# A relational graph layer on one core: message tiles that SyncE fetched row by row are gathered by GpSimd again

## The chip, the cores and the metric

The kernel runs on one core of a Trainium2 chip. The metric is the time of one execution on the device in microseconds (us). Five engines take part, each with its own queue of instructions: PE (TensorE, matrix products; PEld is its loading of weights), DVE (VectorE), ACT (ScalarE), POOL (GpSimd) and SP (SyncE, which here only issues transfers). Transfers (DMA) run beside them on 16 DMA engines and are issued from SP's queue and from POOL's.

## The reference

12,500 nodes with 256 features each; 212,500 edges, sorted by the node they lead to (`dst`), of which the last one of each node is its loop to itself; each edge has one of 8 types. Layer norm and relu, then one weight matrix per type, then a sum over the edges into each node, and a residual:

```python
def _L0_gnn_ref(edge_index, x, edge_type, weight, h_bias, loop_weight):
    src, dst = (edge_index[0], edge_index[1])
    hx = jnp.einsum('ni,rio->rno', x, weight)
    msg = hx[edge_type, src]
    agg = jax.ops.segment_sum(msg, dst, num_segments=num_nodes)
    node_repr = agg * jnp.asarray(ALPHA, x.dtype) ** 0.5
    node_repr = node_repr + h_bias
    loop_message = x @ loop_weight
    node_repr = node_repr + loop_message * jnp.asarray(1.0 - ALPHA, x.dtype) ** 0.5
    return node_repr

h = jnp.maximum(_layernorm(x, axis=-1), 0.0)
x = x + _L0_gnn_ref(edge_index, h, edge_type_8, L0_gnn_weight, L0_gnn_h_bias, L0_gnn_loop_weight)
```

## The kernel before

The kernel sums first and multiplies later: for every node and every type it adds up the normalized rows `h` of the sources, and only these sums meet the weights.

**Tiles.** An edge tile is 128 edges, one per partition. Two tiles make a unit (`PAIR = 2`), 128 units make a block of indices. There are 1603 tiles, 802 units and 7 blocks. From the second block on a unit covers 267 consecutive edges: the loop edges at the ends of nodes are taken out and come in by another way (`begin`, L799), and the others are moved together into the unit's 256 places. `prepare(b)` (L624) does this for one block on DVE, a few instructions per tile, starting 184 tiles ahead of the block's first tile; it leaves, among others, `gidx[b]`, the source rows of the block's tiles, one column of 128 row numbers per tile.

**Gather.** `gather(t)` (L687) brings the 128 source rows of tile t, 1 KB each, into a message buffer: one indirect transfer issued by POOL (L703), with a column of `gidx` as row numbers. The first 96 tiles read raw `x` rows and normalize them on the spot, since the table `h32` in DRAM isn't complete yet; all others read `h32`. The buffers are pairs of tiles, `MSGS // PAIR` = 30 of them. The main loop calls `gather(t + AHEAD)` at tile t with `AHEAD = 58`, so a gather takes the buffer of the pair 30 pairs earlier, and POOL waits there until PE has read it.

**The single rows.** For one tile in 64 (t % 64 = 63, from the second block on, except the last 58 tiles: tiles 319, 383, ..., 1535, 20 in all) `gather` issues nothing on POOL. It puts eight jobs into the list `fetches`, one for each 16 rows. `load_sources` (L707) loads 16 row numbers from `single[b]`, a copy of the second halves of the units' sources, into registers of SP (L710), and puts 16 transfers of one row each into the list, each addressed by a register (L714). `fetch(3)` (L717, called at L1068) does three entries of the list at each tile.

**Sums.** `onehots(t)` (L721) makes the 0/1 matrices of four tiles on DVE by comparing the edges' places with a row of numbers. `edge_sums(t)` (L747) multiplies the message rows with them on PE into `ps` (L757; four matmul records per tile), and `add_sums(u)` (L765) adds a unit's `ps` to a ring of sums in SBUF, `acc`, on DVE (L769).

**Products.** When the last unit of a group of 128 nodes is in, `group_work(g)` (L904) puts 18 products (L917, 36 records) with the weights into a queue. The main loop spreads them over the following tiles; `finish` (L925) adds the rows of `x` and stores the result from SP's queue (L931, L934).

**Order.** Everything is issued in program order by the loop `for t in range(NT)` from L1064, and each engine works its queue in that order. SP's queue holds the index loads, the row loads of `x` and `h` for groups of nodes (L873), the stores of results and the single rows.

Of the kernel before, what the change touches and what calls it, by code (L numbers as in the profile page):

```python
# [11 lines left out]
I32 = mybir.dt.int32  # L12
# [6 lines left out]
DVE = mybir.EngineType.DVE  # L19

P = 128
SP = mybir.EngineType.SP
EPS = 1e-5
ALPHA = 0.5

# [14 lines left out]
CLEARED = 3  # L40
RING = GROUP * SLOTS

MSGS = 60
AHEAD = 58


# [10 lines left out]

ROWS = 6
FIRST = 4


SINGLE = 64
FETCH = 3
SOURCES = 16

LATE = 8

# [148 lines left out]
def kernel(  # L216
# [11 lines left out]
    nc = tc.nc  # L228
    N, D = x.shape
# [7 lines left out]
    NT = plan.NT  # L237
    U = PAIR * P
# [11 lines left out]
    h32 = dram.tile([N, D], F32, name="h32")  # L250
# [20 lines left out]
    def place_of(t):  # L271
        u, i = divmod(t, PAIR)
        return u // P, i, u % P


    with ExitStack() as main:
# [6 lines left out]
        idx = main.enter_context(tc.tile_pool(name="idx", bufs=2))  # L283
        cols = main.enter_context(tc.tile_pool(name="cols", bufs=3))
        small = main.enter_context(tc.tile_pool(name="small", bufs=4))
        msgs = main.enter_context(tc.tile_pool(name="msgs", bufs=MSGS // PAIR))
        ohs = main.enter_context(tc.tile_pool(name="ohs", bufs=2 + LEAD // QUAD))
# [14 lines left out]

        outs = [ps_o.tile([P, 2, D], F32, name=f"po{i}") for i in range(2)]
        msg, oh, offsets, kind = {}, {}, {}, {}
        single, fetches = {}, []
        firsts, stops, loops, marked, typed, gidx, col = {}, {}, {}, {}, {}, {}, {}
        added, zeroed = {}, {}
        state = {"h32": None}
# [28 lines left out]
        def turned(got, cols, to):  # L337

            def turn():
                pt = ps_d.tile([P, 512], F32, tag="pt", name="ptr")  # L340
                for i in range(PAIR):
                    half = slice(i * P, (i + 1) * P)
                    nc.tensor.transpose(pt[:, half], got[cols][:, half], ident)  # L343
                nc.vector.tensor_copy(to(), pt[:, :U])  # L344

            return [turn]

        def work_tile(got, name, tag, dtype=F32, n=EDGES):
            got[name] = ep.tile([P, n], dtype, tag=f"work{tag}", name=name)
            return got[name]  # L350

        def compacted(got, bit, bits):

            def step(k):
                m = work_tile(got, "moves", 5, I32)
                nc.vector.tensor_single_scalar(m, packed, 1 << (bit + k), op=ALU.bitwise_and)  # L356
                nc.vector.copy_predicated(  # L357
                    packed[:, : EDGES - (1 << k)], m[:, 1 << k :], packed[:, 1 << k :])

            return [lambda k=k: step(k) for k in range(bits)]  # L360

        def kept_sources(b, got):

            def keep():
                single[b] = idx.tile([P, P], I32, name="single")
                nc.vector.tensor_copy(single[b], got["sf"][:, P:U])

            return [] if b == 0 else [keep]

        def sources(b, got):  # L370


            if b == 0:
                def copy():
                    nc.vector.tensor_copy(work_tile(got, "sf", 2)[:, :U], got["s"][:, :U])

                return [copy, *turned(
                    got, "sf", lambda: gidx.setdefault(b, idx.tile([P, U], I32, name="gidx")))]

            def rises():  # L380
                nc.vector.tensor_tensor(
                    work_tile(got, "rise", 0), got["d"][:, 1:], got["d"][:, :EDGES], op=ALU.subtract)

            def stays():
                nc.vector.tensor_scalar(
                    work_tile(got, "stay", 1), got["rise"], 0.0, None, op0=ALU.is_equal)
                firsts[b] = small.tile([P, 1], F32, name="firsts")
                nc.vector.tensor_copy(firsts[b], got["d"][:, 0:1])

            def shifts():  # L390
                nc.vector.scalar_tensor_tensor(
                    work_tile(got, "code", 2), got["d"][:, :EDGES], firsts[b], got["stay"],
                    op0=ALU.subtract, op1=ALU.mult)

            def codes():
                nc.vector.scalar_tensor_tensor(
                    got["code"], got["code"], float(R), got["t"][:, :EDGES], op0=ALU.mult, op1=ALU.add)

            def packs():
                nc.vector.scalar_tensor_tensor(  # L400
                    packed, got["s"][:, :EDGES], float(1 << (TB + SB)), got["code"],
                    op0=ALU.mult, op1=ALU.add)

            def unpacks():
                nc.vector.tensor_single_scalar(
                    work_tile(got, "from", 5, I32)[:, :U], packed[:, :U], TB + SB,
                    op=ALU.logical_shift_right)
                nc.vector.tensor_scalar(  # L408
                    work_tile(got, "sf", 2)[:, :U], got["from"][:, :U], 0.0, float(N - 1),
                    op0=ALU.max, op1=ALU.min)  # L410
                nc.vector.tensor_single_scalar(
                    work_tile(got, "rest", 3, I32)[:, :U], packed[:, :U], (1 << (TB + SB)) - 1,
                    op=ALU.bitwise_and)

            return [rises, stays, shifts, codes, packs, *compacted(got, TB, SB), unpacks,
                    *turned(got, "sf", lambda: gidx.setdefault(b, idx.tile([P, U], I32, name="gidx"))),
                    *kept_sources(b, got)]

        def last_edges(b, got):

# [203 lines left out]
        def prepare(b):  # L624

            got = {}
            return [
                lambda: got.update(load_indices(b)), *sources(b, got), *last_edges(b, got),
                *columns(b, got), *places(b, got), *(verdict(got) if b == NB - 1 else [])]
# [57 lines left out]
        def gather(t):  # L687
            if t % PAIR == 0:
                both = msgs.tile([P, PAIR, D], F32, name="msg")
                for i in range(PAIR):  # L690
                    msg[t + i] = both[:, i, :]
            if t % QUAD:
                kind[t] = kind[t - 1]
            else:
                kind[t] = "h" if state["h32"] is not None and t >= state["h32"] + LATE else "x"
            table = {"h": h32, "x": x}[kind[t]]
            b, i, u = place_of(t)
            if b and i and kind[t] == "h" and t % SINGLE == SINGLE - 1 and t + AHEAD < NT:
                for r in range(0, P, SOURCES):
                    fetches.append(lambda r=r: load_sources(t, r))  # L700
                return
            at = i * P + u
            nc.gpsimd.indirect_dma_start(  # L703
                out=msg[t], out_offset=None, in_=table[:, :],
                in_offset=bass.IndirectOffsetOnAxis(ap=gidx[b][:, at : at + 1], axis=0))

        def load_sources(t, r0):  # L707

            b, _, u = place_of(t)
            _, vals = nc.values_load_multi_w_load_instructions(  # L710
                single[b][u : u + 1, r0 : r0 + SOURCES], engines=[SP], min_val=0, max_val=N - 1,
                skip_runtime_bounds_check_because="clamped to the table where they are computed")
            for i, v in reversed(list(enumerate(vals))):
                fetches.insert(0, lambda i=i, v=v: nc.sync.dma_start(  # L714
                    msg[t][r0 + i : r0 + i + 1, :], h32[bass.ds(v, 1), :]))

        def fetch(n):  # L717
            for _ in range(min(n, len(fetches))):
                fetches.pop(0)()

        def onehots(t):  # L721

# [140 lines left out]
        got = {}  # L863
# [98 lines left out]
        with tc.manual_schedule():  # L962
# [16 lines left out]
            nc.vector.memset(ones_b, 1.0)  # L979
            nc.vector.memset(zero, 0.0)  # L980
            head = len(sources(0, {}))
            for f in load[1 : 1 + head]:
                f()
            for t in range(min(AHEAD, NT)):
                gather(t)
# [49 lines left out]
            def blocks_ahead(t):  # L1035
                for b in range(1, NB):
                    if t == max(0, U * b - PREP):
                        for k, f in enumerate(prepare(b)):
                            background.append((t + STEP * (k // OPS), f))
                        background.sort(key=lambda a: a[0])  # L1040
# [23 lines left out]
            for t in range(NT):  # L1064
                done["tile"] = t
                if t + AHEAD < NT:
                    gather(t + AHEAD)
                fetch(FETCH)  # L1068
                blocks_ahead(t)
                for f in after:  # L1070
                    f()
# [30 lines left out]
                while queue and (budget > 0 and t >= queue[0][0] or t >= queue[0][1]):  # L1102
                    _, _, c, f = queue.pop(0)
# [4 lines left out]
                while waiting and (len(waiting) > LAG or t == NT - 1):  # L1108
                    u, ps = waiting.pop(0)
# [54 lines left out]
```

## Time and profile before

| | |
|---|---|
| time, median of 3 runs | 2032.05 us (2030.82 to 3686.84) |
| time of the profiled execution | 2030.82 us |
| its span, first to last instruction | 2029.1 us |
| granted TensorE clock, mean over the span | 0.945 |
| gathers by POOL (L703) | 96 of `x` and 1487 of `h32` |
| single rows by SP (L714) | 2560 transfers of 1.0 KB, 160 register loads (L710) |
| DMA queues, share of 16 engines' span | 35.0% POOL's, 11.1% SP's |

The profile is one execution, recorded by the hardware profiler. A busy time is the time in which an engine executes an instruction; what its sequencer does for itself (waiting, branching, handing a transfer over) isn't counted as busy. "idle before, releaser" is the time in which the engine stood before an instruction, and what ended it; "issue" there means that the profile shows nothing that it waited for. A row of a timeline gives the start, the duration, the instruction, and the idle time ahead of it in brackets.

### The profile page before, as it was taken

How to read it: one execution, taken by the hardware profiler on the slowest of the kernel's cores; microseconds unless marked ns; L12 is line 12 of the kernel's file. 1: busy time of each engine (PE TensorE's matmuls, PEld its weight loads, DVE VectorE, ACT ScalarE, POOL GpSimd, SP SyncE). 2: the span in 40 equal slices, each digit the busy share in tenths (PEclk: the TensorE clock that was granted, in tenths of full speed). 3: DMA queues.
4: the chain of work that ended last, by engine and by line, in shares of the span. 5: the costliest groups of instructions: out<-in, count | busy, mean ns of one | idle time of the engine just before them, and what ended most of it. 6: DMA issues, size and time to landing. Idle time of an engine off the chain costs nothing.

```text
span 2029.1 us, 37425 instructions
## 1 busy us (share of the span) xinstructions
PE 1784.7 (88%) x10411; PEld 1627.0 (80%) x10411; DVE 1324.2 (65%) x3281; ACT 218.4 (11%) x470; POOL 1504.2 (74%) x1609
## 2 busy tenths in 40 slices
PE   2458999997999997999997989897998898899998
PEld 2357899987989886989886989776898787788886
DVE  7859666658666659656568666557665567765642
ACT  7855110000000000000000000000000000000000
POOL 7757777777777777777777777777777777777773
PEclk8569999998999998999998999999999999999999
DMA  8973443444444444444444444434344444444442
GB/s 293 374 224 105 140 125 117 139 128 125 129 138 120 138 134 121 127 140 118 129 138 127 128 118 138 129 117 146 112 133 129 118 139 130 118 138 123 119 119 72
DMA packets 151127, 281.70 MB, mean 139 GB/s; under 512 B 30365, under 2 KB 100260, under 8 KB 150916
## 3 DMA queue, kind: packets, MB, share of 16 engines
q0 software_dynamic: 75984, 207.59, 35.0%
q1 hardware_dynamic: 74932, 71.68, 11.1%
q8 instruction: 85, 1.39, 0.3%
q14 instruction: 126, 1.03, 0.2%
HBM read 253.55 MB, written 25.60 MB: 138 GB/s over the span
## 4 chain that ended last, share of the span: by engine, by line
PE 33%; SPq 24%; issue 14%; DMA 11%; DVE 11%; POOL 4%; ACT 2%; DVEq 0%; ACTq 0%; POOLq 0%
SPq L714 19%; PE ps L757 17%; PE po L917 15%; DMA msg<-h,gidx 5%; SPq L710 5%; POOL msg L703 4%; DVE acc L769 2%; DMA xr<-in_x_dram 1%; DVE moves L356 1%; DVE fixed L357 1%; DMA h<-xt 1%; DVE oh L730 1%; DMA hr<-h 1%; DVE acc L807 1%; DMA msg<-h 1%
## 5 line engine op out<-in xcount | busy, mean ns | idle before, releaser
L703 POOL DMA_INDIRECT msg<-h,gidx x1487 | 1411.4, 949 | 467.8 <-issue 387.2
L757 PE MATMUL ps<-oh,msg 128*128 128x176 f32 (+1 forms) x6412 | 1151.5, 310 | 168.9 <-ACT msg L661 62.8
L757 PEld LDWEIGHTS ps<-oh,msg 128*128 128x128 f32 x6412 | 1047.5, 197 | 287.8 <-issue 84.2
L917 PE MATMUL po<-w,acc 128*128 128x256 f32 x3136 | 890.6, 386 | 0.0
L730 DVE TENSOR_TENSOR oh<-fixed,cols 128x704 f32<-128x704 f32 x402 | 355.8, 886 | 337.7 <-PE ps L757 328.3
L917 PEld LDWEIGHTS po<-w,acc 128*128 128x128 f32 x3136 | 543.3, 194 | 28.6 <-issue 5.2
L769 DVE TENSOR_TENSOR acc<-acc,ps 128x352 f32 x802 | 412.9, 515 | 158.6 <-PE ps L757 147.7
L807 DVE SCALAR_TENSOR_TENSOR acc<-types,pst 128x256 f32<-128x256 bf16 (+1 forms) x688 | 234.9, 414 | 95.5 <-ACT self_t L796 94.4
L796 ACT ACTIVATE self_t<-pst 128x256 f32<-128x256 f32 x98 | 37.4, 382 | 1470.5 <-PE pst L793 1470.5
L703 POOL DMA_INDIRECT msg<-in_x_dram,gidx x96 | 90.9, 947 | 31.1 <-issue 25.6
L917 PE MATMUL po<-wl,self_t 128*128 128x256 f32 x392 | 106.6, 396 | 3.9 <-ACT self_t L796 2.4
L917 PEld LDWEIGHTS po<-wl,self_t 128*128 128x128 f32 x392 | 70.0, 199 | 10.3 <-ACT self_t L796 2.8
L661 ACT ACTIVATE xt<-xt,n_shift,n_rstd 128x256 f32<-128x256 f32 x98 | 50.9, 588 | 11.0 <-DVE n_shift L658 11.0
L661 ACT ACTIVATE msg<-msg,e_shift,e_rstd 128x256 f32<-128x256 f32 x96 | 49.6, 588 | 8.6 <-DVE e_shift L658 8.6
L928 DVE TENSOR_TENSOR xr<-xr,po 128x256 f32<-128x256 f32 x98 | 40.4, 412 | 7.8 <-PE po L917 7.8
L852 ACT ACTIVATE diagonal<-ident,kinds 128x128 bf16<-128x128 f32 x88 | 28.1, 390 | 149.7 <-DVE kinds L849 149.7
L929 DVE TENSOR_TENSOR xr<-xr,po 128x256 f32<-128x256 f32 x98 | 41.2, 421 | 3.4
L793 PE MATMUL pst<-ident,hr 128*128 128x128 f32 x196 | 38.8, 281 | 1.7 <-DVE cols L344 1.7
L356 DVE TENSOR_SCALAR moves<-fixed 128x267 int32<-128x267 int32 x84 | 36.3, 432 | 1.6
L357 DVE COPY_PREDICATED fixed<-moves,fixed 128x266 int32<-128x266 int32 (+6 forms) x84 | 33.7, 401 | 2.9
L649 DVE BATCH_NORM_STATS2 n_stats<-xt 128x6 f32<-128x256 f32 x98 | 34.4, 411 | 0.9 <-issue 0.7
L343 PE MATMUL ptr<-ident,sf 128*128 128x128 f32 x14 | 4.5, 421 | 33.5 <-DVE sf L408 30.2
(201 smaller groups left out, 351.6 us busy)
## 6 DMA issues: line engine op xcount, KB each, us to landing
msg<-h SPq DMA_DIRECT2D x2560, 1.0 KB
msg<-h,gidx POOLq DMA_INDIRECT x1487
xt<-in_x_dram SPq DMA_DIRECT2D x24, 512.0 KB
h<-xt SPq DMA_DIRECT2D x24, 512.0 KB
xr<-in_x_dram SPq DMA_DIRECT2D x24, 512.0 KB
hr<-h SPq DMA_DIRECT2D x24, 512.0 KB
out_dram<-xr SPq DMA_DIRECT2D x24, 512.0 KB
w<-in_L_gnn_weight_dram SPq DMA_DIRECT2D x2, 1024.0 KB
```

The lines of the kernel that those rows point to most:

```text
L356: nc.vector.tensor_single_scalar(m, packed, 1 << (bit + k), op=ALU.bitwise_and)
L357: nc.vector.copy_predicated(packed[:, : EDGES - (1 << k)], m[:, 1 << k :], packed[:, 1 << k :])
L661: nc.scalar.activation(rows_[j], rows_[j], AF.Relu, bias=shift[:n, j : j + 1], scale=rstd[:n, j : j + 1])
L703: nc.gpsimd.indirect_dma_start(out=msg[t], out_offset=None, in_=table[:, :], in_offset=bass.IndirectOffsetOnAxis(ap=gidx[b][:, at : at + 1 ...
L710: _, vals = nc.values_load_multi_w_load_instructions(single[b][u : u + 1, r0 : r0 + SOURCES], engines=[SP], min_val=0, max_val=N - 1, skip ...
L714: fetches.insert(0, lambda i=i, v=v: nc.sync.dma_start(msg[t][r0 + i : r0 + i + 1, :], h32[bass.ds(v, 1), :]))
L730: nc.vector.tensor_tensor(o[:, k : k + v, :i, :], iota_f.unsqueeze(1).unsqueeze(1).to_broadcast([P, v, i, C]), of.unsqueeze(3).to_broadcas ...
L757: nc.tensor.matmul(ps[:, c, from_ : from_ + width], m[:, c * P : (c + 1) * P], o[:, :width], start=(i == 0 and c == 0), stop=(end and c == ...
L769: i = nc.vector.tensor_tensor(a, a, ps, op=ALU.add)
L807: i = nc.vector.scalar_tensor_tensor(acc[:, :, r, s0 : s0 + n], of, float(r + 1), pst[:, :, :n], op0=ALU.is_equal, op1=ALU.mult)
L917: i = nc.tensor.matmul(got["out", g][:n], lhs, rhs, start=(r == R and c == 0), stop=(r == R - 1 and c == KC - 1))
L929: nc.vector.tensor_add(rows_[:n, k, :], rows_[:n, k, :], got["out", g][:n])
```

## The change

Three things. The tiles with t % 64 = 63 are no longer an exception: `gather` issues an indirect transfer on POOL for each of the 1603 tiles. With the single rows go `load_sources`, `fetch`, the list, and the six copies `single`. And `MSGS` is 62 in place of 60, which makes 31 message buffers of two tiles; `AHEAD` stays 58.

```diff
-MSGS = 60
+MSGS = 62
 AHEAD = 58
...
-SINGLE = 64
-FETCH = 3
-SOURCES = 16
...
-        def kept_sources(b, got):
-
-            def keep():
-                single[b] = idx.tile([P, P], I32, name="single")
-                nc.vector.tensor_copy(single[b], got["sf"][:, P:U])
-
-            return [] if b == 0 else [keep]
...
-                    *turned(got, "sf", lambda: gidx.setdefault(b, idx.tile([P, U], I32, name="gidx"))),
-                    *kept_sources(b, got)]
+                    *turned(got, "sf", lambda: gidx.setdefault(b, idx.tile([P, U], I32, name="gidx")))]
...
-            if b and i and kind[t] == "h" and t % SINGLE == SINGLE - 1 and t + AHEAD < NT:
-                for r in range(0, P, SOURCES):
-                    fetches.append(lambda r=r: load_sources(t, r))
-                return
...
-        def load_sources(t, r0):
-
-            b, _, u = place_of(t)
-            _, vals = nc.values_load_multi_w_load_instructions(
-                single[b][u : u + 1, r0 : r0 + SOURCES], engines=[SP], min_val=0, max_val=N - 1,
-                skip_runtime_bounds_check_because="clamped to the table where they are computed")
-            for i, v in reversed(list(enumerate(vals))):
-                fetches.insert(0, lambda i=i, v=v: nc.sync.dma_start(
-                    msg[t][r0 + i : r0 + i + 1, :], h32[bass.ds(v, 1), :]))
-
-        def fetch(n):
-            for _ in range(min(n, len(fetches))):
-                fetches.pop(0)()
...
-                fetch(FETCH)
```

In the built program PE and ACT execute the same numbers of instructions, DVE six fewer, POOL 20 gathers more (1507 of `h32`), and SP 198 rows of instructions where it had 5478.

More of the change, by code (lines that the diff above doesn't have):

```diff
@@ L21 @@
 P = 128
-SP = mybir.EngineType.SP
 EPS = 1e-5
@@ L304 @@
         msg, oh, offsets, kind = {}, {}, {}, {}
-        single, fetches = {}, []
         firsts, stops, loops, marked, typed, gidx, col = {}, {}, {}, {}, {}, {}, {}
```

## The prediction

> **What bounds the kernel now.** The page comes first: which engine is busiest, and what chain of work ended last.
>
> ```profile
> PE 1784.7 (88%) x10411; PEld 1627.0 (80%) x10411; DVE 1324.2 (65%) x3281; ACT 218.4 (11%) x470; POOL 1504.2 (74%) x1609
> ...
> PE 33%; SPq 24%; issue 14%; DMA 11%; DVE 11%; POOL 4%; ACT 2%; DVEq 0%; ACTq 0%; POOLq 0%
> ```
>
> Read by these lines, PE is the bound, SP's queue (the single rows) carries a quarter of the chain, and POOL hardly matters. Both are to be doubted. Busy is not the same as occupied: handing over a transfer isn't counted. And the chain follows one releaser at each step, so a tile that came from SP leads it into SP's queue for as long as SP was issuing. The test is whether an engine ever waits for another. So the second view is POOL's timeline, in the middle of the run, where nothing is special:
>
> ```profile
> 601.99 0.95 POOL L703 DMA_INDIRECT msg<-h,gidx  x1 [0.30 <-issue]
> 603.24 0.95 POOL L703 DMA_INDIRECT msg<-h,gidx  x1 [0.30 <-issue]
> 604.49 0.94 POOL L703 DMA_INDIRECT msg<-h,gidx  x1 [0.30 <-issue]
> 605.74 0.95 POOL L703 DMA_INDIRECT msg<-h,gidx  x1 [0.30 <-issue]
> ```
>
> A gather starts every 1.25 us: 0.95 busy, 0.30 of handing over. The third view, POOL's waits from 250 us to 2003 us (total, times, longest), says whether it is ever more than that:
>
> ```profile
> POOL msg L703 <- issue: 360.5, 1183, 0.3
> POOL msg L703 <- PE ps L757: 39.9, 131, 0.3
> POOL msg L703 <- DMA msg<-h,gidx: 13.1, 43, 0.3
> ```
>
> No wait is longer than 0.3 us, so the engines named there hold nothing up: from 250 us on POOL gathers without a pause. Whether PE depends on it shows in the records made up to a time; the first four rows are POOL's gathers, the others PE's tile matmuls at L757, four per tile:
>
> ```profile
> 0.00:250.00 250.00, 174.57 (x185) 0.76 0.71 229
> 0.00:800.00 800.00, 591.11 (x623) 0.90 0.53 160
> 0.00:1700.00 1700.00, 1272.22 (x1341) 0.94 0.48 143
> 0.00:2000.00 2000.00, 1499.40 (x1580) 0.94 0.47 140
> ```
> ```profile
> 0.00:250.00 250.00, 113.63 (x528) 104.21 (x528) 0.76 0.71 229
> 0.00:800.00 800.00, 444.47 (x2436) 412.92 (x2437) 0.90 0.53 160
> 0.00:1700.00 1700.00, 974.10 (x5421) 892.28 (x5422) 0.94 0.48 143
> 0.00:2000.00 2000.00, 1147.20 (x6388) 1043.65 (x6388) 0.94 0.47 140
> ```
>
> At 250 us 185 tiles are gathered and 528/4 = 132 are multiplied: 53 in stock. At 800 us it is 623 and the 5 tiles from SP so far, less 609: 19. At 1700 us 1341 + 17 - 1355 = 3, at 2000 us 1580 + 20 - 1597 = 3. Between 250 and 800 us PE takes 1908/4 = 477 tiles, one per 1.15 us, while POOL makes one per 1.25. PE eats the stock up and then goes at POOL's pace. **POOL's issue of gathers is the bound of the whole run**; PE's 88% is what its work looks like when it is fed just in time.
>
> After the last gather comes a tail:
>
> ```profile
> 2002.87 0.95 POOL L703 DMA_INDIRECT msg<-h,gidx  x1 [0.30 <-issue]
> ...
> 2004.20 0.83 PE L757 MATMUL ps<-oh,msg 128*128 128x176 f32 x4 [0.43 <-DMA msg<-h,gidx]
> ...
> 2016.71 7.07 PE L917 MATMUL po<-w,acc 128*84 128x256 f32 x32
> ```
>
> From 2004.20 on PE has the products of the last groups before it; they, an addition and a store end at 2029.1. So the run is: first gather at 4.76, 1582 intervals between gathers, and 2029.1 - 2002.87 = 26.2 us of tail; the execution's own time is 1.7 us more than its span (2030.8).
>
> **Part by part.** *20 more gathers on POOL.* From the gather at 251.12 us to the one at 367.36, before SP issues its first single row, 93 intervals take 1.250 us each; from 1917.84 to 2002.87, after the last one, 68 take 1.250. The 20 additional ones each lie on the path, since nothing else is late on it: 20 x 1.250 = **+25.0 us**. They pull 2.6 MB over from SP's queue to POOL's; the 16 engines are about 45% busy in this stretch, so the bytes are costed at nothing.
>
> *The single rows off SP's queue.* 2560 transfers, each with two register instructions ahead (0.22 + 0.04 + 0.03 us), and 160 loads of 1.28 us: 0.74 + 0.20 ms of SP's time. SP waits for nobody on the path; behind its rows stood only the index loads, the group rows and the stores. The index loads matter to POOL through `gidx`, but the closest case has it written at 187.8 us for a gather at 339.9. PE waited 30.4 us in 8 places for single rows (longest 6.1); that goes, but PE is faster than POOL by 0.1 us per tile and has made the wait good within some 60 tiles; the last such tile, 1535, lies 67 ahead of the end. So this is worth nothing in itself. What may be worth something is the disturbance of POOL: between 369.86 and 1915.33 us its 1232 intervals average 1.2544, and its few long ones (a gather of 1.48 us instead of 0.95 at 475.13) lie in this stretch alone. 1232 x 0.0044 = 5.4 us. That the rows cause it isn't shown, only the coincidence in time; the bounds are 0 and -5.4. I take **-4**, nearer to the undisturbed rows on both sides.
>
> *31 buffers instead of 30.* POOL is held where PE hasn't freed a buffer yet; this is early, while the weights load:
>
> ```profile
> 134.97 0.94 POOL L703 DMA_INDIRECT msg<-h,gidx  x1 [5.34 <-ACT e_rstd L653]
> ...
> 142.89 0.94 POOL L703 DMA_INDIRECT msg<-h,gidx  x1 [5.73 <-issue]
> ```
>
> These and three smaller holds (1.02, 1.41 and 2.65 us of idle time, the last ending at 222.15) make 16.15 - 5 x 0.30 = 14.7 us. The releaser named is wrong, but the buffers fit: the hold at 222.15 is for tile 162, and PE's last matmul of tile 103, the former owner, ends at 221.88. With one pair more this gather waits for tile 101, which ended at 215.96. One pair of buffers lets POOL be two gathers further when PE frees the next; it doesn't make PE free them sooner. Going through all gathers with the release times of this trace moved by one pair, the gather of tile 256 starts at 337.0 instead of 339.5. **-2.5 us**; the bounds are 0 and the whole 14.7. From 250 us on the stock is below 58 and more buffers are worth nothing.
>
> *Six copies off DVE*, 0.24 us each: 1.4 us of an engine busy 65%, beside POOL; nothing. *The tail* stays: the same products in the same order, and PE's pace there is its own.
>
> Sum: 25.0 - 4 - 2.5 = **+18.5 us**; 2030.8 + 18.5 = 2049.3 for an execution like the profiled one. The median of the three runs is 1.2 us above it: **2050 us**, 0.9% more.
>
> Two rules of the Trainium skill stand against each other here. *DMA: Bandwidth & Descriptors*, "Issuing engines are not separate DMA queues", says that issuing from several engines saves only the sequencer's time to initiate a transfer, usually little beside the transfer itself. By it the change would cost about nothing and the sum would be -6.5. The trace has the opposite case: the initiation is 1.25 us and is the run's pace. *Perfetto Trace Analysis*, "DMA Optimizations", says that where descriptor generation is the bottleneck, balancing over the issuing engines may help. That speaks against this change, which takes a balance away, and by it the sum is the one above.
>
> **The rivals.** *SP's rows and PE are the bound, and the run gets faster.* For it: SP's queue at 24% of the chain, PE at 88%, 30.4 us of PE waiting for single rows. Then these 30.4 us go, and 3.2 us of PEld: 2030.8 - 33.6 = 1997. Against it: 1603 gathers at 1.250 from 4.76 us on, with no hold at all, put the last one at 2007.3, and the tail ends the execution at 2035. To come under the 2030.8 of before POOL would have to keep below 1.247 us per gather with no hold; for a gain of 2% below 1.222. No quiet stretch shows that. Chance 0.03.
>
> *POOL becomes slower per gather, and the run is slower by more than 2%.* Place: the software queue, which now carries every row after 320 us and has PE only some 3 tiles behind. If POOL has to wait there for the queue to drain or for a buffer, every following gather shifts. Price: from +18.5 to +2% (40.6 us) it takes 22 us, 14 ns on each of 1603 gathers. For it: that little is enough, and intervals of 1.3 to 1.8 us exist. Against it: they occur only while SP issues rows, and the stretch without them after 1917 us, also at a stock of 3, has 1.250. Chance 0.07; about 2075.
>
> *The cost is hidden early.* If the one additional pair dissolved all five holds and the disturbance went whole, 25.0 - 14.7 - 5.4 = +4.9: 2036 to 2037. It needs PE to free buffers sooner in the first 220 us, which the change doesn't touch. Chance 0.06.
>
> **How the numbers follow.** The forecast has 0.84. Its own range goes from both credits a little larger (2045) to both at nothing: 2030.8 + 25.0 + 1.2 = 2057. Down to 2044 and up to 2058 takes in the edge of the neighbours and should hold the time 8 times in 10. 2% either way, about what a measurement of this kernel can tell from no change, are 1991 and 2073: faster 0.03, slower 0.07, within 0.90.
>
> **What would show it.** After: 1603 gathers at L703's successor; intervals of 1.250 without the long ones, from 250 us to the end; the hold at 222 us gone or shorter, and the gather of tile 256 near 337 us; the last gather near 2021 us and 26 us of tail behind it; PE's stock empty sooner than before 1100 us; no SP in the chain, but POOL or its transfers. It is wrong if the last gather is before 2015 us, if intervals exceed 1.26 us in the mean, or if the tail isn't 26 us.

## The result and the profile after

The changed kernel takes 2049.23 us, the median of 6 runs (2047.77 to 2052.66); the kernel before, over all its runs beside it, 2031.35. The ratio is 1.0097, with a 95% interval of 1.0082 to 1.0111: slower by 1%, where the prediction had 2050 us and 0.9%. The ratio is that of the mean times, and one run of the kernel before, at 3686.84 us, is left out of it. The profiled execution of the changed kernel is its fastest, 2047.77 us with a span of 2046.1; 17.0 us more span than the profiled one before.

The experiments further down all fell on three chips on which the kernel before takes 2696 to 2735 us instead of 2031; on which chip the comparison above ran is not on record. Each is compared with the kernel before on the same chip, and most of them answered another question than the one that they were made for.

First the page of the changed kernel: busy time of each engine, and the chain of work that ended last.

```profile
PE 1795.5 (88%) x10411; PEld 1602.1 (78%) x10411; DVE 1324.3 (65%) x3275; ACT 218.4 (11%) x470; POOL 1522.6 (74%) x1629
...
PE 50%; DMA 15%; DVE 12%; issue 11%; POOL 8%; ACT 3%; DVEq 0%; SPq 0%; ACTq 0%; POOLq 0%
```

The shares of busy time are those of before within two points (PEld 78% for 80%, the others to the per cent): nothing here would tell that the run is slower. SP's queue, which had 24% of the chain, has none. Taking it out of the chain made the run no faster, which settles how that 24% was to be read: the tiles came from SP by that way, but the time was not spent there.

The second view is POOL's waits from 250 us to the last gather (total, times, longest):

```profile
POOL msg L683 <- issue: 354.0, 1162, 0.3
POOL msg L683 <- PE ps L723: 52.7, 173, 0.3
POOL msg L683 <- DMA msg<-h,gidx: 9.8, 32, 0.3
```

Again none is longer than 0.3 us: POOL gathers without a pause, as before. The stock of tiles comes from the records made up to a time, POOL's gathers (L683) first, PE's tile matmuls (L723, four per tile) after them:

```profile
0.00:250.00 250.00, 179.72 (x190) 0.79 0.71 232
0.00:800.00 800.00, 596.00 (x629) 0.92 0.52 160
0.00:2000.00 2000.00, 1504.40 (x1586) 0.96 0.46 139
```
```profile
0.00:250.00 250.00, 114.53 (x545) 104.33 (x546) 0.79 0.71 232
0.00:800.00 800.00, 447.94 (x2469) 412.67 (x2470) 0.92 0.52 160
0.00:2000.00 2000.00, 1145.30 (x6336) 1018.12 (x6336) 0.96 0.46 139
```

190 - 136 = 54 tiles at 250 us, 629 - 617 = 12 at 800 (19 before), 1586 - 1584 = 2 at 2000. The stock is used up sooner: between 250 and 800 us 439 tiles come in, all by POOL, where both ways together brought 443, and PE takes 481 instead of 477. PE waits more for gathers, as its waits over the whole run show (81.3 us, 132 times; before 38.0, 60 times):

```profile
PE ps L723 <- DMA msg<-h,gidx: 81.3, 132, 4.2
```

The fourth view is POOL's timeline where it was held before, and the end of the run:

```profile
130.09 0.95 POOL L683 DMA_INDIRECT msg<-h,gidx  x1 [0.30 <-ACT msg L645]
131.34 0.95 POOL L683 DMA_INDIRECT msg<-h,gidx  x1 [0.30 <-issue]
133.18 0.94 POOL L683 DMA_INDIRECT msg<-h,gidx  x1 [0.90 <-ACT e_rstd L637]
134.43 0.94 POOL L683 DMA_INDIRECT msg<-h,gidx  x1 [0.30 <-issue]
140.51 0.94 POOL L683 DMA_INDIRECT msg<-h,gidx  x1 [5.13 <-issue]
...
2020.23 1.09 POOL L683 DMA_INDIRECT msg<-h,gidx  x1 [0.30 <-issue]
```
```profile
2030.90 0.76 PE L723 MATMUL ps<-oh,msg 128*128 128x176 f32 x4
...
2034.05 7.07 PE L883 MATMUL po<-w,acc 128*84 128x256 f32 x32
```

The hold of 5.34 us ahead of the gather at 134.97 is gone; that gather, tile 100, now starts at 130.09, without one. Of the two long holds before (5.34 and 5.73 us, tiles 100 and 102) one is left, 5.13 us ahead of tile 104. The last gather starts at 2020.23 instead of 2002.87, and 25.8 us after it the run ends (26.2 before).

The whole difference can be put together from the starts of the gathers in the two traces. First gather: 0.1 us later. 20 gathers more at 1.250: +25.0. Intervals beyond 1.250 up to the gather of tile 185: 15.1 us before, 8.4 after, so -6.7. The same from there to the end: 5.5 and 4.5, so -1.0. Sum +17.4, which is the 2020.23 - 2002.87. The tail gives back 0.4.

### The profile page after: what moved, and what is told of

Its sections match the earlier page's. It is cut to its first block, busy times and chain, and to the rows that moved or that the text cites. A ratio compares the mean times of both kernels' runs of the same rounds, so it can differ in the third digit from the quotient of the medians.

```text
span 2046.1 us, 29386 instructions
## 1 busy us (share of the span) xinstructions
PE 1795.5 (88%) x10411; PEld 1602.1 (78%) x10411; DVE 1324.3 (65%) x3275; ACT 218.4 (11%) x470; POOL 1522.6 (74%) x1629
## 4 chain that ended last, share of the span: by engine, by line
PE 50%; DMA 15%; DVE 12%; issue 11%; POOL 8%; ACT 3%; DVEq 0%; SPq 0%; ACTq 0%; POOLq 0%
PE ps L723 27%; PE po L883 22%; DMA msg<-h,gidx 12%; POOL msg L683 8%; DVE acc L735 2%; DVE acc L773 2%; DVE moves L349 1%; DMA h<-xt 1%; DVE fixed L350 1%; ACT xt L645 1%; DVE oh L696 1%; PE pst L759 1%; DMA w<-in_L_gnn_weight_dram 1%; ACT msg L645 0%; DVE n_stats L633 0%
## 5 line engine op out<-in xcount | busy, mean ns | idle before, releaser
L683 POOL DMA_INDIRECT msg<-h,gidx x1507 | 1429.7, 949 | 466.9 <-issue 380.2
L723 PE MATMUL ps<-oh,msg 128*128 128x176 f32 (+1 forms) x6412 | 1159.2, 310 | 185.3 <-DMA msg<-h,gidx 81.3
L723 PEld LDWEIGHTS ps<-oh,msg 128*128 128x128 f32 x6412 | 1029.9, 195 | 340.3 <-issue 68.5
L683 POOL DMA_INDIRECT msg<-in_x_dram,gidx x96 | 90.9, 947 | 31.2 <-issue 25.0
L633 DVE BATCH_NORM_STATS2 e_stats<-msg 128x6 f32<-128x256 f32 x96 | 33.5, 412 | 0.0
```

What stands on the lines that cost most here:

```text
L633: nc.vector.bn_stats(stats[:n, j, :], rows_[j])
L683: nc.gpsimd.indirect_dma_start(out=msg[t], out_offset=None, in_=table[:, :], in_offset=bass.IndirectOffsetOnAxis(ap=gidx[b][:, at : at + 1 ...
L723: nc.tensor.matmul(ps[:, c, from_ : from_ + width], m[:, c * P : (c + 1) * P], o[:, :width], start=(i == 0 and c == 0), stop=(end and c == ...
```

## The experiments

**e1 to e4** were to test the bound and the buffers.

```diff
e1   -MSGS = 62
     +MSGS = 60
e2   +            if b and i and kind[t] == "h" and t % 64 == 63 and t + AHEAD < NT:
     +                nc.scalar.activation(msg[t], zero.to_broadcast([P, D]), AF.Copy)
     +                return
e3   -            for r in [R, *range(R)]:
     +            for r in [R, *range(R // 2)]:
     ...
e4   -MSGS = 62
     -AHEAD = 58
     -LATE = 8
     +MSGS = 56
     +AHEAD = 54
     +LATE = 12
```

> The changed kernel with 30 pairs of message buffers instead of 31 (MSGS = 60), nothing else. The profile of the changed kernel has its gather of tile 256 start at 333.3 us where before had 339.9: 6.6 us gained early, where the prediction had 2.5. Theory A (a pair of buffers is worth two gathers, and the rest of the 6.6 is other variation of the start): 2.5 us slower than the changed kernel, 2051.7 us, ratio to before about 1.011, the gather of tile 256 near 336. Theory B (one pair is worth the whole 6.6, because PE too gets ahead): 2056 us, ratio 1.0125 or more, the gather of tile 256 near 340. Both: everything after 250 us at 1.25 us per gather, as in the changed kernel.

> The changed kernel, but the 20 tiles that SP had fetched before (319, 383, ..., 1535) are neither gathered nor fetched: ScalarE writes zeros to their buffers, so their messages are left out of the sums. Theory (POOL's issue sets the pace, each gather 1.25 us on the path, SP's rows worth nothing): 25.0 us less than the changed kernel, 2024 us, ratio to before 0.9965; gathers still 1.250 us apart, PE a few tiles behind them. Rival (PE is the bound and the rows only delay it): no more than 3 us off the changed kernel, 2046 to 2049. Second question, the long gathers (26 of over 1.29 us in the changed kernel after 250 us, 4.5 us in all): if SP's rows made them they would be gone in the changed kernel already; expected here as there, 4 to 5 us in all.

> The changed kernel with the products of four of the eight types left out (1568 of 3136 records on L883, 887 us of PE's work halved); the output misses these types. Theory (POOL is the bound): the last gather stays at 2020 us within 3 us, and only the tail of products behind it gets shorter, by about half of its 16 us: 2041 us, ratio to before 1.005. PE's busy share falls to about 66% with no gain. Rival (PE at 88% is the bound): 440 us less work gives 1610 to 1700 us.

> The changed kernel with 28 pairs of message buffers instead of 31 (MSGS = 56, AHEAD = 54, and LATE = 12 so that the same 96 tiles read x). Theory A of e1 (two gathers per pair): 7.5 us more than the changed kernel, 2056.7. Theory B (6.6 per pair): 20 us more, 2069. The stock of tiles ahead of PE is empty sooner, with no further price. Rival: the stock matters later too (PE runs dry at the boundaries of index blocks), over 2070.

Measured, beside 2734.74 us of the kernel before on the same chip: e1 2519.41 (ratio 0.9206, 0.9179 to 0.9232), e2 2497.39 (0.9123, 0.9091 to 0.9155), e3 2492.72 (0.9123, 0.9086 to 0.9159), e4 2517.32 (0.9198, 0.9167 to 0.9229). None of the numbers expected can be met, since the run is of another kind there. DVE's timeline in the first microseconds shows it, of the changed kernel first and then of e1; of the four aggregates of a norm (L635) the second to the fourth start late in e1, two of them by the signal of an instruction before on the same engine:

```profile
20.32 0.36 DVE L635 BATCH_NORM_AGGREGATE n_mv<-n_stats 128x2 f32<-128x6 f32 x4
```
```profile
20.54 0.18 DVE L635 BATCH_NORM_AGGREGATE n_mv<-n_stats 128x2 f32<-128x6 f32 x1
21.94 0.18 DVE L635 BATCH_NORM_AGGREGATE n_mv<-n_stats 128x2 f32<-128x6 f32 x1 [1.22 <-DVE n_mv L635]
23.34 0.18 DVE L635 BATCH_NORM_AGGREGATE n_mv<-n_stats 128x2 f32<-128x6 f32 x1 [1.21 <-DVE n_mv L635]
24.74 0.18 DVE L635 BATCH_NORM_AGGREGATE n_mv<-n_stats 128x2 f32<-128x6 f32 x1 [1.22 <-issue]
```

Four in 0.36 us there, one in 1.40 us here. The instructions themselves take about as long (0.15 to 0.16 us there, 0.18 here); by the releaser named, what comes late is the signal. And POOL is not held up by its own work in e1: by 1000 us it has 640 gathers out and PE has 2342/4 = 585 tiles done, a stock of 55.

```profile
0.00:1000.00 1000.00, 607.80 (x640) 0.86 0.43 129
```
```profile
0.00:1000.00 1000.00, 467.33 (x2342) 417.93 (x2343) 0.86 0.43 129
```

So on this chip POOL has nearly all its buffers filled (55 of 60) and is held by them, and neither the question of e3 (is PE the bound where POOL seems to be) nor that of e1 and e4 (what are buffers worth at the start) can be answered. Half the products less is worth 27 us here (e3 against e1), and four buffers less nothing (e4 against e1: 2 us). One thing doesn't fit a full stock: 20 gathers less, in e2, are worth 22 us against e1.

**e5 to e7** were the kernels of e1 to e3 once more, in the hope of a chip like that of the comparison.

> The kernel of e1 once more. In e1 to e4 the kernel before took 2735 us instead of 2031, and the profile shows why nothing can be told apart there: after a result of one engine the next instruction that needs it starts 1.2 us or more later (the four aggregates of a norm 1.40 us apart instead of 0.1), so POOL was not the bound. If the kernel before takes about 2031 here: theory A (a pair of buffers is worth two gathers) 2051.7 us, ratio to before 1.011, the gather of tile 256 near 336 us; theory B (the whole early gain of 6.6 us comes from the pair) 2056 us, ratio 1.0125 or more, the gather of tile 256 near 340 us.

> The kernel of e2 once more: 20 tiles neither gathered nor fetched, zeros from ScalarE in their place, so their messages are left out of the sums. Where the kernel before takes about 2031: theory (POOL is the bound, 1.25 us on the path per gather) 2024 us, ratio 0.9965; rival (PE is the bound) 2046 to 2049.

> The kernel of e3 once more: the products of four of the eight types left out. Where the kernel before takes about 2031: theory (POOL is the bound) the last gather at 2020 us within 3 us, and 2041 us in all, ratio 1.005; rival (PE is the bound) 1610 to 1700 us.

They fell on the same chip: 2517.76 (ratio 0.9196, 0.9169 to 0.9224), 2493.28 (0.9103, 0.9071 to 0.9135) and 2489.86 (0.9111, 0.9077 to 0.9144), with 2734.53 before. So these times repeat within some 4 us, and the 22 to 24 us of the 20 gathers with them.

**e8** is the kernel before, unchanged, for a profile on the same chip.

> The kernel before once more, unchanged, for a second profile. Where it takes about 2031 us: the last gather at 2003 us within 3, 1.25 us per gather; the gather of tile 256 tells how much the start differs between two executions of one kernel: within 1 us of 339.9 if the 6.6 us gained by the changed kernel come from its buffers, several us off if the start varies by itself. Where it takes about 2735, as beside e1 to e7: the profile shows where the 217 us over e1 lie. Theory: each single row is issued and signalled apart, and where signals are slow SP needs far more than 0.29 us per row, so that PE waits for the fetched tiles, some 10 us for each of the 20. Rival: nothing is late in SP's queue and the time is spread over all tiles.

2740.11 us. PE's longest wait, in total (us, times, longest):

```profile
PE ps L757 <- DMA msg<-h: 266.4, 18, 18.7
```

In the comparison this was 30.4 us in 8 places. In the traces SP's rows of one tile take 63 to 71 us from the first to the last there, and 87 to 104 us here (row to row 0.41 and 0.67 us in the median). The tile is due 58 tiles after it is asked for, which is some 88 us at the pace of e1. So the rows come late by some 15 us, 18 times of 20. This is what the first rival of the prediction supposed, that SP's rows delay PE, on a chip where POOL is not the bound; and there the change (with 30 pairs of buffers, e1) makes the kernel 8% faster instead of 1% slower.

**e9 and e10** asked whether that lateness is the price of the rows.

```diff
e9   -SINGLE = 64
     +SINGLE = 128
e10  -                    fetches.append(lambda r=r: load_sources(t, r))
     +                    q, e, d = (fetches, SP, nc.sync) if r < P // 2 else (others, ACT, nc.scalar)
     +                    q.append(lambda r=r, q=q, e=e, d=d: load_sources(t, r, q, e, d))
     ...
```

> The kernel before with one tile in 128 fetched row by row instead of one in 64 (SINGLE = 128): 10 tiles by SP, 10 more gathered by POOL. Two theories for two conditions. Where the kernel before takes about 2031 us POOL's issue is the bound: 10 gathers more cost 12.5 us, 2044 us, ratio to before 1.006. Where it takes about 2735, PE waits some 15 us for each fetched tile, because SP needs 97 us for its 128 rows and the tile is due 58 tiles after it is asked for, about 88 us: half of these waits go, half of the 217 us between before and e1, 2625 us, ratio 0.96. Rival there (the time between before and e1 comes from something else, such as the number of instructions or the buffers): no more than 30 us off before, or all of the 217.

> The kernel before, but of each fetched tile ScalarE's queue issues rows 64 to 127 and SP's the first 64. Where the kernel before takes about 2031: POOL's gathers are the same, so nothing changes beyond 4 us, ratio 0.998 to 1.002. Where it takes about 2735: the rows of a tile take some 50 us instead of 97, which is inside the 88 us until PE needs them; the waits of PE for single rows go, 2500 to 2520 us, ratio 0.92, at or a little under e1. Rival: ScalarE's own work, behind which PE's products wait (self_t), is held up by the rows, and what is won is lost again: 2600 or more.

A second chip, with 2695.56 us before. e9: 2590.20, ratio 0.9605 (0.9554 to 0.9657), as expected for half the rows. e10: 2669.48, ratio 0.9879 (0.9821 to 0.9937), far from the 0.92 expected. Yet its rows are in time: in the trace the 64 rows of each queue take 43 to 58 us, the last ones are issued 30 to 50 us before PE comes to the tile, and PE has no wait for single rows any more among its longest:

```profile
PE ps L760 <- issue: 281.7, 160, 17.8
PE ptt L837 <- DVE acc L810: 103.9, 12, 16.1
PE ps L760 <- ACT msg L662: 69.4, 10, 32.4
```

What has grown is "issue", which names nothing (189.6 in e8, on the other chip), and a wait on ScalarE, the rival in the expectation (DVE's L810 waits 273.3 us for `self_t`, where e8 has 83.2). So e10 doesn't decide. Either PE's waits were only where the time showed, and taken away there it shows elsewhere; or they were its cause, and what was won was lost again on ScalarE, which now issues rows.

**A count that fits.** The page gives the number of DMA packets under 512 B; first the kernel before (e8), then e1, then e2:

```profile
DMA packets 151127, 281.70 MB, mean 103 GB/s; under 512 B 30365, under 2 KB 100260, under 8 KB 150916
```
```profile
DMA packets 146904, 281.17 MB, mean 112 GB/s; under 512 B 28125, under 2 KB 95460, under 8 KB 146756
```
```profile
DMA packets 145945, 278.56 MB, mean 112 GB/s; under 512 B 27805, under 2 KB 95140, under 8 KB 145796
```

20 gathers less are 320 packets less: 16 small packets to each gather, and, since e1 has 20 gathers more than before and 2560 rows less (-2240 = 320 - 2560), one to each row. In the traces nearly all of them have 4 bytes, and on POOL's queue in e1 there are 25,648 of these, 16 times its 1603 gathers. That they are the signals of completion is a reading. It agrees with the Trainium skill, *DMA: Bandwidth & Descriptors*, section "Why a DMA increments its semaphore by 16 and not by 1": on the software path all 16 engines post their increment, whatever the shape. If each small packet has one price, every kernel so far that does all the work of PE must give it (e3 and e7 don't):

| against before on the same chip | small packets | us | ns for each |
|---|---|---|---|
| e1, 20 gathers for 2560 rows | -2240 | -215.3 | 96 |
| e4, the same | -2240 | -217.4 | 97 |
| e2, the 20 tiles not fetched at all | -2560 | -237.4 | 93 |
| e9, 10 gathers for 1280 rows | -1120 | -105.4 | 94 |
| e10, the rows on two queues | 0 | -26.1 | |

Four that agree, though e1 and e4 are nearly one point. And e10, which moves rows without saving any, stays near before. **e11 and e12** are two more points, one with more of each kind. Their expectations were written before this count was made, from the two earlier ideas.

```diff
e11  -MSGS = 62
     +MSGS = 60
     +            if b and kind[t] == "h" and t % 16 == 15 and t + AHEAD < NT:
     +                nc.gpsimd.indirect_dma_start(
     +                    out=spare, out_offset=None, in_=table[:, :],
     +                    in_offset=bass.IndirectOffsetOnAxis(ap=gidx[b][:, at : at + 1], axis=0))
e12  -            if b and i and kind[t] == "h" and t % SINGLE == SINGLE - 1 and t + AHEAD < NT:
     +            if b and i and kind[t] == "h" and t % (SINGLE // 2) == SINGLE // 2 - 1 and t + AHEAD < NT:
     +                first = t % SINGLE == SINGLE - 1
     +                q, e, d = (fetches, SP, nc.sync) if first else (fetches2, ACT, nc.scalar)
     ...
```

> The changed kernel with 30 pairs of buffers (as e1) and 80 gathers more: at every 16th tile from 271 to 1535 POOL issues the tile's gather a second time, into a tile that nobody reads. The sums are the same. POOL-bound theory, where the kernel before takes about 2031 us: 80 x 1.25 = 100 us over the kernel of e1 (2049 to 2056), so 2149 to 2156, ratio to before 1.06; rival (PE is the bound, gathers are hidden): under 10 us more, 2066 at most. Where the kernel before takes about 2700: POOL has 53 tiles and more in stock there, so if only the place on POOL's queue counts, 0 to 15 us over e1's ratio of 0.92; if a gather costs its 1.2 us in another way even there, as e2 against e1 suggests (20 gathers less, 22 us less), about 90 us more, ratio 0.95.

> The kernel before, and beside SP's tiles (t % 64 = 63) ScalarE's queue fetches the tiles t % 64 = 31 row by row in the same way: 40 tiles off POOL instead of 20. POOL-bound theory, where the kernel before takes about 2031: 25 us less, 2006, ratio 0.988; it would be the fastest version. Rival there: ScalarE's own work (self_t) is held up behind its rows and PE waits: 2031 or more. Where the kernel before takes about 2700: the rows cost there (e8, e10), so slower than before: ratio 1.03 to 1.08.

A third chip, with 2699.46 us before. e11: 2598.00, ratio 0.9621 (0.9589 to 0.9654); e12: 2953.85, ratio 1.0947 (1.0910 to 1.0983). Their small packets, e11 first:

```profile
DMA packets 150745, 291.67 MB, mean 112 GB/s; under 512 B 29405, under 2 KB 96740, under 8 KB 150596
```
```profile
DMA packets 155350, 282.23 MB, mean 96 GB/s; under 512 B 32605, under 2 KB 105060, under 8 KB 155076
```

e11 has 960 fewer than before and takes 101.5 us less: 106 ns for each. e12 has 2240 more and takes 254.4 us more: 114 ns. So six kernels on three chips, with changes of both signs, give 93 to 114 ns per small packet against the kernel before. None of the six changes gathers alone. The one pair that does, e2 against e1, gives less: 22.0 us for 320 packets, 69 ns (76 in e6 against e5). Bytes and instructions don't do this: e11 moves 10 MB more than before and is faster, and of the instructions saved by e1 it gives back only those of 80 gathers, but about half of the time (though on another chip). It remains a fit, and two prices fit as well: 93 ns for a row (e2 against before) and 1.1 us for a gather (e2 against e1), or 1.4 (e11 and e1, each against the kernel before on its own chip), which is about POOL's 1.25 us. No run changed the number of signals and left the transfers alone, and the 2560 rows that e12 adds are issued by ScalarE, whose own work they may delay.

What stays open: the direct test of the bound where the kernel before takes 2031 us. e2, e3, e11 and e12 were made for it, and none met that condition. A kernel that asks POOL for fewer and larger gathers, which the theory would make faster there, wasn't tried either; so no version is shown to beat the kernel before there.

## Why the prediction was right

**The bound, and 20 gathers at 1.250 us.** This carried the forecast, and the pair of profiles agrees in each point that it named: no wait of POOL over 0.3 us after 250 us, 1.250 in all but a few intervals, the stock empty sooner, the tail unchanged (25.8 us for 26.2), SP gone from the chain with nothing won. An engine that never stands longer than its 0.3 us between two gathers, from 250 us to its last one, with a tail of nearly the same length behind it, is the path in both executions, and 20 gathers more lengthen it by 20 intervals; the 25.0 us stand in the difference of the last gathers beside terms read off separately. This rests on these two executions; the experiments neither confirm nor shake it.

**The credit for the single rows, -4, was mis-sized: -1.0.** The step said that intervals over 1.25 us lie only where SP issues rows, and took the coincidence for a likely cause. In the changed kernel SP issues none, and 26 intervals over 1.29 us are still there between 383 and 1901 us (35 before), such as this gather of 1.24 us, with what DVE does beside it:

```profile
1176.96 1.24 POOL L683 DMA_INDIRECT msg<-h,gidx  x1 [0.30 <-issue]
```
```profile
1176.86 0.53 DVE L865 TENSOR_TENSOR acc<-acc 128x352 f32<-128x352 f32 x1
1177.52 0.35 DVE L868 MEMSET acc<- 128x352 f32 x1
```

Nine of the 26 stand at the same tile as a long one before or at the next (tile 1051, 1441 and 1507, for instance). So they belong to something that both programs do, and the traces show what lies beside them. SP's large transfers don't. But all 26 long gathers overlap in time with a DVE instruction of `mark` (14, L788), of `prepare` (10) or of `wrap` (2, L865 and L868); of the other gathers after 250 us an eighth does. In the kernel before, 34 of its 35 do. That these instructions lengthen a gather fits, but no run moved them.

**The credit for the buffers, -2.5, was right, and the start gave more: -6.7 in all up to tile 185.** Going through the changed kernel's gathers with its own release times, 31 pairs put the gather of tile 256 at 333.2 (it is at 333.3), and 30 pairs at 335.7. So the pair is worth 2.5 us there too, and the other 4.2 come from PE, which frees buffers earlier: tile 25 starts 0.8 us sooner than before, tile 40 1.8, tile 110 4.6. The lead exists at tile 25, at 88 us, before any buffer was short, so the additional pair isn't its beginning. Its largest step, 3.5 us, comes between tiles 101 and 103; the kernel before is shown first, then the changed one:

```profile
217.70 0.54 PE L793 MATMUL pst<-ident,hr 128*128 128x128 f32 x2 [1.74 <-DVE cols L344]
...
218.89 1.38 PE L757 MATMUL ps<-oh,msg 128*128 128x176 f32 x4
```
```profile
214.77 0.38 PE L759 MATMUL pst<-ident,hr 128*128 128x128 f32 x2
...
215.43 0.76 PE L723 MATMUL ps<-oh,msg 128*128 128x176 f32 x4
```

Before, PE stood 1.74 us for DVE there, and the clock granted to it was 0.50 from 218 to 221 us; in the changed kernel it didn't stand there, and the clock was 1.00 (over the first 250 us 0.76 before and 0.79 after, in the rows above). Whether the change makes this lead or two executions differ that much wasn't settled: e1 and e4 were to say so and couldn't. The runs of each kernel spread by 5 us (five of the six before, all six after), which leaves room for it.

The two errors are of opposite sign, +3 and -4, and that is why the sum came out within 1 to 2 us: 18.5 forecast, 17.0 between the profiled executions, 17.9 between the medians. That closeness is luck: each of the two terms alone was off by 3 to 4 us.

**SP's time was priced too low.** The working has 0.29 us per row and 0.94 ms in all, from the durations of the instructions. By the starts in the same trace a row takes 0.41 us and a tile 63 to 71, about 1.3 ms for the 20. The total does not depend on it, since SP is not on the path.

**The rivals.** The first, SP's rows and PE are the bound, didn't happen in the comparison, and its floor (1603 gathers at 1.250 us) held. On a chip where POOL was not the bound the run did get faster, by 8% (e1), far more than the 33.6 us that the rival was priced at. Whether by the mechanism that it named is open: e10 took PE's waits away and won 1%, but delayed ScalarE. The second rival, more than 1.25 us per gather with an empty stock, didn't happen: 1.253 in the mean. The third needed PE to free buffers sooner in the first 220 us. That did happen, but it was worth 4 us, and with the pair 6.7 of the 14.7.

## What to carry to other kernels

Take an engine for the bound when nothing ever makes it wait and the run ends a fixed tail after it, whatever its busy share or its share of the chain: POOL was 74% busy and 4% of the chain, and 20 steps of 1.25 us more on its queue moved its last gather by 25.0 us, beside what changed at the start. A wait that names a transfer tells where time shows, which need not be what it is spent on; a test has to move the transfer, and without loading another engine as e10 did. And an exchange of one resource for another, here POOL's issue against SP's rows, has a sign only for the condition under which it was measured: the change was 1% slower where the kernel before takes 2031 us and, with one pair of buffers less, 8% faster where it takes 2735.

## What the runs showed that was not expected

- The kernel before took 2031 us in the comparison and 2696 to 2740 beside the experiments; the changed one took 2049, and with 30 pairs of buffers 2518 to 2519 there. In the profiles of the experiments DVE's aggregates that wait for a signal start late, most of them by 0.5 or by 1.2 us (both stand in e2), from about 20 us on; up to then (the first 18 us) DVE's instructions of e1 and of the changed kernel stand at the same times within 0.1 us. The traces of the experiments also hold fewer separate semaphore updates from DMA (7,995 in e1, 28,119 in the changed kernel, for the same number of 4-byte packets, 28,123), as if they came in bundles. The cause of the condition wasn't found.
- In that condition a tile fetched row by row cost 237.4 / 20 = 11.9 us (e2 against before), and a gathered one 22.0 / 20 = 1.1 us (e2 against e1).
- A row fetched from a register address cost SP 0.41 us from row to row in the comparison, and 16 row numbers 1.28 us to load: 63 us or more per tile, which PE takes in 1.15 to 1.25 us. In these runs that was worth it only where the queue that is relieved was the bound.
